# A macaron network on one core: KAN input made once and copied by transfers, rotated query by transfers, one ring of PSUM banks

## The chip, the cores and the metric

The kernel runs on one core of one Trainium2 chip. The metric is the device time of one execution in microseconds (us); the time of the kernel before is the median of three runs. The engines that matter are PE (TensorE, matmuls), DVE (VectorE), ACT (ScalarE), POOL (GpSimd), and the queue SP, from which most transfers (DMAs) are issued, one after the other.

## The reference, cut to what matters

Sixteen sequences ("rows", b = 0 to 15) of 512 tokens with 128 features pass five residual blocks: a KAN block, causal attention with rotary positions, the same KAN block again, an expert block, and a recurrence with a second expert block. The change touches the first three.

```
x = x + 0.5 * ffn(layernorm(x))      # KAN
x = x + attn(layernorm(x))           # 16 query heads of 8, 4 key heads, causal
x = x + 0.5 * ffn(layernorm(x))      # KAN

ffn:  s = x @ Win + bin               # 128 -> 64
      h = relu(s[..., None] * W1 + b1)   # 16 hidden values for each of the 64
      g = (h * W2).sum(-1) + b2
      out = g @ Wout + bout              # 64 -> 128
attn: q = x @ Wq;  q = q * cos + rotate_half(q) * sin
      rotate_half swaps the two halves of a head's 8 values and negates one
```

Every KAN needs each of its 64 inner features 16 times, with another slope and offset each time.

## The kernel before, in words

**Staging.** The program is a set of Python generators. Each `yield` ends a turn; `turn()` lets every live generator run one step and so fixes the order of the instructions on PE, DVE, ACT and POOL, which then run in that order. Only the SP queue is ordered by a scheduler. While a row runs (`paced`), a generator asks for room in the turn with `need(...)`, and `bank(...)` hands out one of two PSUM banks ("mm") for side work. Work appended to `later` is issued at the start of the next turn.

**The main loop** goes through rows b = -1 to 15 in 44 turns each: `weights(b)` makes the transposed scores of row b on PE (L713, tile `ps_st`), ACT takes their exponent (L716, `pt`) and POOL cuts the diagonal (L718); `maxima(b+1)` makes the scores of the next row (L649, `ps_sc`) and DVE takes their row maxima (L654, L659). `outputs` multiplies weights by values (L739, `ps_av`). Beside these, as side work, run `stage_in(b+2 and on)` (first KAN, then `attn_in`: query, key and value) and `stage_out(b-1)` (output product, second KAN, gate scores). Row -1 has maxima alone. Before it stands a prologue: loads, KANs of rows 0 to 2, `attn_in` of rows 0 and 1. Behind row 15 come 512 products of experts (L1026 `ps_h`, L1039 `ps_y`, L990 `acc`), a PE-filled stage of some 660 us, with `recurrence` beside it.

**`kan(b)`.** After `norm` (DVE statistics, POOL power, transposes L338, ACT copy L340 to `kan_xT`) it makes the input product twice, once for each half of the 64 features, with a weight `win` that holds the 32 columns four times side by side: one 128x512 float32 matmul for each half (L358, `ps_s`; two passes of PE each), copied by ACT to `kan_s0` and `kan_s1` (L361). So the 128 partitions hold 32 features four times. Eight ACT instructions (L377, `kan_h`) spread over 15 turns give two of the hidden values for 64 features each. Eight matmuls of 32 columns (L387, `ps_kg`) sum them, four column groups of PE side by side; then ACT copy (L393), product with `wout` (L401, `ps_ko`), sum on DVE (L402).

**`attn_in(b)`.** Two 128x512 matmuls give the query (L445, `ps_pa`, weight `wq`) and the query with each head's halves swapped (L451, `ps_pb`, weight `wqr`); DVE multiplies them by cosine and sine (L446, L452), POOL adds them (L467). `parts` splits the sum into three bf16 parts, which go to DRAM (L427, `qs`) and come back in the layout of the scores (L516, `qp`).

**PSUM.** Eight banks: two "mm", one `avp`, one `kap` and two `scp` for the maxima in turn, two `stp` for the weights. So the maximum in turn i waits for DVE to have read that of turn i-3, and the weight of turn i waits for ACT to have read that of turn i-2. In row 15 the weights use the two `scp` banks too. In the expert stage `kap` holds `ps_x`, `scp` `ps_h` and `stp` `ps_y`.

**SP's first transfers** in order: x of row 0 (L72), `win`, small weights, `rope` (L188), x of rows 1 to 15 (L72), `wo` (L195), `wlam` (L217), `wf` (L219), `wst` (L1082), and then the transfers of `attn_in`.

Of the kernel before, what the change touches and what calls it, by code (L numbers as in the profile page):

```python
# [17 lines left out]
P = 128  # L18
# [19 lines left out]
IN, OUT = 38, 8  # L38
LATE = 28
EP = 5  # L40
PLACES = 8
# [7 lines left out]
def tile_macaron(  # L49
# [55 lines left out]
    with ExitStack() as ph:  # L105
# [8 lines left out]
        avp = ph.enter_context(tc.tile_pool(name="p1_av", bufs=1, space=PSUM))  # L114
        kap = ph.enter_context(tc.tile_pool(name="p1_ka", bufs=1, space=PSUM))
        scp = ph.enter_context(tc.tile_pool(name="p1_sc", bufs=2, space=PSUM))
        stp = ph.enter_context(tc.tile_pool(name="p1_st", bufs=2, space=PSUM))
        qkp = ph.enter_context(tc.tile_pool(name="qk", bufs=1))
# [6 lines left out]
        nc.vector.tensor_scalar_add(center, ident, -1.0 / D)  # L125
        win = cst.tile([D, 2, NI, MH], F32, name="win")
        binc = cst.tile([P, 2], F32, name="binc")
# [8 lines left out]

        for half in range(2):
            cols = win_in[:, half * MH : (half + 1) * MH]
            nc.sync.dma_start(out=win[:, half, :, :], in_=cols.unsqueeze(1).to_broadcast([D, NI, MH]))
        inner(kw1, kw1_in)  # L140
# [38 lines left out]

        wq = cst.tile([D, NH, HD], F32, name="wq")  # L180
        nc.sync.dma_start(out=wq, in_=wq_in.rearrange("k (h d) -> k h d", d=HD))
        wk = cst.tile([D, 2, HD, NR], F32, name="wk")
# [4 lines left out]
        rope = cst.tile([P, 2, S], F32, name="rope")  # L187
        nc.sync.dma_start(out=rope, in_=rope_in)  # L188
        out_weights()
# [6 lines left out]
        hh = HD // 2  # L196
        wqr = cst.tile([D, NH, HD], F32, name="wqr")
        identb = cst.tile([P, P], BF16, name="identb")
# [59 lines left out]

        held, kan_held, hurry = [0], [0], [False]

        def bank(shape, dtype, name, work=0.0):
# [8 lines left out]
        def freed():  # L270
            held[0] -= 1
# [77 lines left out]
        def kan(b):  # L349

            _, xT = yield from norm(x[b])
            sk = []
            for half in range(2):
                while half and kan_held[0]:
                    yield
                kan_held[0] |= half
                ps = yield from bank([P, S], F32, "ps_s", 0.9)
                nc.tensor.matmul(ps, lhsT=win[:, half, :, :].rearrange("d i m -> d (i m)"), rhs=xT,  # L358
                                 start=True, stop=True)
                sh = (w1p if half else w2p).tile([P, S], F32, name=f"kan_s{half}")  # L360
                later.append(lambda sh=sh, ps=ps: nc.scalar.copy(sh, ps))  # L361
                yield
                take(act=0.6)
                freed()
                sk.append(sh)
            yield

            hs = []
            begin = now[0]
            U = 2 * NV  # L370
            for t in range(U):
                while now[0] < begin + 15 * t // 8:
                    yield
                yield from need(act=0.8, **({"pool": 1.25} if t == 1 else {}))
                half, v = t // 2 % 2, t // 4 * 2 + t % 2
                h = hp.tile([P, S], F32, name="kan_h")
                nc.scalar.activation(h, sk[half], AF.Relu, bias=rbias[:, half, v : v + 1],  # L377
                                     scale=kw1[:, half, v : v + 1])
                hs.append((half, v, h))
                if t == 1:  # L380
                    nc.gpsimd.tensor_tensor(x[b], x[b], kcst.unsqueeze(1).to_broadcast([P, NT, D]), ALU.add)
                yield
            pg = yield from bank([P, S], F32, "ps_kg", 1.0)
            for begins in (True, False):
                for half, v, h in hs[0:4] if begins else hs[4:8]:
                    o = half * M + v % 2 * MH
                    nc.tensor.matmul(pg[o : o + MH, :], lhsT=w2d[:, half, v, :], rhs=h,  # L387
                                     start=begins, stop=not begins)
                if begins:
                    yield  # L390
                    yield from need(pe=1.0)
            gT = w2p.tile([P, S], F32, name="kan_g", tag="kan_s0")
            later.append(lambda: nc.scalar.copy(gT, pg))  # L393
            kan_held[0] = 0
            yield
            take(act=0.6)
            freed()
            yield
            po = yield from bank([P, NT, D], F32, "ps_ko", 0.9)
            for c in range(NT):  # L400
                nc.tensor.matmul(po[:, c, :], lhsT=gT[:, bass.ts(c, P)], rhs=wout, start=True, stop=True)  # L401
            later.append(lambda: nc.vector.tensor_add(x[b], po, x[b]))  # L402
            yield
            take(dve=0.7)
            freed()
            yield
# [16 lines left out]
        def spread(part, heads, name):  # L423

            scr = tc.dram_tile([3, HD, heads, S], BF16, name=name)
            for i in range(3):
                nc.sync.dma_start(out=scr[i].rearrange("d h t -> h d t"), in_=part[:, i, :])  # L427
            return scr
# [8 lines left out]
        def attn_in(b, st):  # L437
            _, xT = yield from norm(x[b])
            ka = w1p.tile([P, 2, P], F32, name="rope_ka")
            ta = w1p.tile([P, S], F32, name="rope_a")  # L440
            tb = w1p.tile([P, S], F32, name="rope_b", tag="yT")
            qpart = w1p.tile([P, 3, S], BF16, name="qpart")
            kpart = w1p.tile([P, 3, P], BF16, name="kpart")
            pa = yield from bank([P, S], F32, "ps_pa", 0.9)
            nc.tensor.matmul(pa, lhsT=wq.rearrange("k h d -> k (h d)"), rhs=xT, start=True, stop=True)  # L445
            later.append(lambda: nc.vector.tensor_mul(ta, pa, rope[:, 0, :]))  # L446
            yield
            take(dve=0.7)
            freed()
            pb = yield from bank([P, S], F32, "ps_pb", 0.9)  # L450
            nc.tensor.matmul(pb, lhsT=wqr.rearrange("k h d -> k (h d)"), rhs=xT, start=True, stop=True)  # L451
            later.append(lambda: nc.vector.tensor_mul(tb, pb, rope[:, 1, :]))  # L452
            yield
            take(dve=0.7)
            freed()
            pkv = yield from bank([P, 3, P], F32, "ps_kv", 1.3)
# [8 lines left out]
            yield  # L465
            yield from need(pool=1.25)
            nc.gpsimd.tensor_tensor(ta, ta, tb, ALU.add)  # L467
            take(dve=0.4)
# [16 lines left out]
            freed()  # L485
            st["va"] = va
            if paced[0]:
                yield
# [40 lines left out]
        def center_win():  # L529
            psc = yield from bank([P, 2 * NI * MH], F32, "ps_kc0")  # L530
            centered(psc, win.rearrange("d a i m -> d (a i m)"))
            freed()
# [10 lines left out]
        def prepare():  # L543
# [24 lines left out]
            psc = yield from bank([P, 3, P], F32, "ps_kc3")  # L568
            centered(psc[:, 0, :], wq.rearrange("k h d -> k (h d)"))
            centered(psc[:, 1, :], wk[:, 0, :, :].rearrange("k d h -> k (d h)"), wk[:, 0, :, :])  # L570
            centered(psc[:, 2, :], wv)
            freed()
            yield
            nc.vector.tensor_copy(wqr[:, :, 0:hh], wq[:, :, hh:HD])
            nc.vector.tensor_copy(wqr[:, :, hh:HD], wq[:, :, 0:hh])
            nc.vector.tensor_copy(wk[:, 1, 0:hh, :], wk[:, 0, hh:HD, :])
# [40 lines left out]
        def stage_in(b, st):  # L617
            late = b in through
            yield from kan_in(b)
            for _ in range(LATE if late and b > 2 else 0):  # L620
# [6 lines left out]
                 (1, (0, 1)), (1, (2, 3)), (0, (0, 1, 2, 3))]  # L627

        def in_bank(ps, gs):
            return ps.rearrange("p (u w) -> p u w", w=S // len(gs))  # L630

        turns = [0]

        def maxima(b, st):
            qp, kp = packed(b)
            for half in range(2):
                maxs = topped[half][:, 0 : NT * NH // 2].rearrange("p (h c) -> p h c", c=NT)
                for r in (2 * half, 2 * half + 1):
                    for c, gs in BANKS:
                        n = (c + 1) * P  # L640
                        v = in_bank((kap if turns[0] % 3 == 2 else scp).tile([P, S], F32, name="ps_sc"), gs)
                        turns[0] += 1
                        alone = len(gs) == 1
# [52 lines left out]
        def weights(b, st):  # L696
# [3 lines left out]
            for r in range(NR):  # L700
                pt = ptp.tile([P, NG, 1280], F32, name="pt")
                st["pt"][r] = pt
                for i, (c, gs) in enumerate(BANKS):
                    c = NT - 1 - c
                    n = S - c * P

                    if b == B - 1 and (r * len(BANKS) + i) % 2:
                        ps = scp.tile([P, S], F32, name="ps_sl", tag="ps_sc")
                    else:
                        ps = stp.tile([P, S], F32, name="ps_st")  # L710
                    v = in_bank(ps, gs)
                    for u, g in enumerate(gs):
# [231 lines left out]
        def dispatch():  # L944
            while taken[0] < NR * B:
                yield
            for i in range(0, len(order), 2):
# [4 lines left out]

                ps = kap.tile([D, 2, CAP], F32, name="ps_x", tag="ps_sc")
                for j in range(2):
# [6 lines left out]
        def experts():  # L961
# [55 lines left out]
            while begun[0] < len(order) or any(line) or rounds:  # L1017
                now = None
                if begun[0] < moved[0]:
# [3 lines left out]
                    begun[0] += 1  # L1023
                    pst = scp.tile([P, NF, CAP], F32, name="ps_h", tag="ps_sc")
                    for f in range(NF):
# [5 lines left out]
                if line[1]:  # L1031
                    k, b, e, u = line[1]
                    g, n = b // GB, (b % GB) * E + e
                    if prod[1]:
                        v = place[k, b, e]
                        nc.vector.tensor_scalar(sels[v], iota, tokT[g][:, n : n + 1], None, ALU.is_equal)  # L1036
                    py = stp.tile([CAP, D], F32, name="ps_y", tag="ps_st")
                    for f in range(NF):
# [273 lines left out]
```

## Time and profile before

| what | value |
|---|---|
| three runs | 1592.62, 1592.74, 1594.12 us; median 1592.74 us |
| the profiled execution | 1585.11 us, span of its instructions 1583.1 us, mean granted PE clock 0.984 |
| busy share of the span | PE 93%, weight loads 66%, DVE 69%, ACT 61%, POOL 58% |
| prologue and row -1, 0 to 110.88 us | up to the first exponent of row 0 |
| rows 0 to 15, 110.88 to 913.11 us | rows 5 to 9 take about 52 us each |
| expert stage, 920 to 1583 us | PE 99% busy up to 1440 us |
| L358 `ps_s`, 128 passes | 71.1 us busy, 644 ns each |
| L361 copies of `ps_s`, 64 | 37.5 us busy, 586 ns each |
| L451 `ps_pb`, 32 passes | 17.5 us busy, 628 ns each |

The times of rows are those between the first exponents of successive rows in the timeline. A line of the profile names the line of the kernel, the engine, and the tiles written and read; "idle" is the time in which the engine had nothing running before an instruction, with what released it. The end of a matmul is modelled, so the distance between the starts of successive matmuls tells more than their durations do.

### The profile page before, as it was taken

To read this page: it belongs to the slowest core of one execution; us is meant where nothing else is said; L and a number is where in the kernel's file an instruction comes from. 1 tells how busy PE (TensorE), PEld (TensorE's weight loads), DVE (VectorE), ACT (ScalarE), POOL (GpSimd) and SP (SyncE) were. 2 spreads that over 40 slices of the span, in tenths; PEclk is the share of its full clock that TensorE was granted. 3 is DMA by queue.
4 is the path that set the end of the run, shared out by engine and by line. 5 is a ranking of instruction groups with operands and counts; after the bars stand their busy time and mean duration, and the time that the engine had idled before them with its cause. 6 is when DMAs were issued, how large, how long until landed. Compare 5 with 4: busy or idle time off the path is not lost.

```text
span 1583.1 us, 33175 instructions
## 1 busy us (share of the span) xinstructions
PE 1479.8 (93%) x11902; PEld 1045.6 (66%) x11905; DVE 1085.0 (69%) x3574; ACT 960.5 (61%) x1852; POOL 922.7 (58%) x1439
## 2 busy tenths in 40 slices
PE   4689989999999999999999899999999999999997
PEld 2334454455445454445444489999998999999997
DVE  5587877878788788888888345765569665753333
ACT  3445767777778777777776865444454444544443
POOL 2535545555555564556454766667666666767773
PEclk9889999999999999999999999999999999999998
DMA  5220110122111210221122113223332332333332
GB/s 136 81 58 30 58 52 13 50 59 60 36 33 53 60 52 12 58 60 35 30 79 68 50 45 70 60 57 73 72 73 59 72 72 63 81 64 67 69 67 60
DMA packets 107466, 92.87 MB, mean 59 GB/s; under 512 B 23469, under 2 KB 95862, under 8 KB 107062
## 3 DMA queue, kind: packets, MB, share of 16 engines
q1 hardware_dynamic: 84464, 67.67, 15.0%
q0 software_dynamic: 21584, 22.89, 7.8%
q8 instruction: 93, 1.52, 0.4%
q14 instruction: 71, 0.58, 0.1%
q10 hardware_dynamic: 1254, 0.20, 0.1%
HBM read 59.20 MB, written 35.45 MB: 60 GB/s over the span
## 4 chain that ended last, share of the span: by engine, by line
PE 76%; DVE 10%; ACT 7%; issue 2%; DMA 2%; POOL 1%; SPq 1%; ACTq 0%; DVEq 0%; POOLq 0%
PE ps_h L1026 13%; PE ps_y L1039 13%; PE ps_av L739 9%; PE ps_st L713 7%; PE ps_sc L649 5%; PE acc L990 5%; PE ps_kg L387 4%; ACT pt L716 4%; PE ps_s L358 3%; DVE below L654 3%; ACT kan_h L377 2%; PE ps_t L338 2%; PE ps_x L955 2%; DVE topped L659 2%; PE ps_g L800 2%
## 5 line engine op out<-in xcount | busy, mean ns | idle before, releaser
L716 ACT ACTIVATE pt<-ps_st 128x512 f32<-128x512 f32 x682 | 369.9, 566 | 126.3 <-PE ps_st L713 124.6
L718 POOL TENSOR_SCALAR_AFFINE_SELECT pt<-pt 128x128 f32<-128x128 f32 (+2 forms) x704 | 250.9, 365 | 320.4 <-ACT pt L716 314.4
L654 DVE CUSTOM_DVE_ANT_0 below<-ps_sc,causal 128x512 bf16<-128x512 f32 (+1 forms) x512 | 315.6, 616 | 106.5 <-PE ps_sc L649 91.0
L935 POOL DMA_INDIRECT xg<-xnd,tokI x256 | 252.8, 988 | 82.9 <-issue 37.8
L1028 ACT ACTIVATE mo<-ps_h 128x512 f32<-128x512 f32 x256 | 152.8, 597 | 217.7 <-PE ps_h L1026 217.4
L713 PE MATMUL ps_st<-qp,kp 128*128 128x512 bf16 (+1 forms) x990 | 247.6, 301 | 33.2 <-ACT pt L716 30.7
L1026 PE MATMUL ps_h<-xin,mw 128*128 128x128 f32 x2048 | 272.5, 276 | 0.0
L1039 PE MATMUL ps_y<-mw,mo 128*128 128x128 f32 x2048 | 270.8, 275 | 0.0
L649 PE MATMUL ps_sc<-kp,qp 96*128 96x512 bf16 (+3 forms) x1024 | 256.6, 304 | 5.9 <-DVE topped L654 3.9
L1026 PEld LDWEIGHTS ps_h<-xin,mw 128*128 128x128 f32 x2048 | 250.3, 192 | 12.4 <-issue 9.9
L1039 PEld LDWEIGHTS ps_y<-mw,mo 128*128 128x128 f32 x2048 | 249.4, 192 | 1.0 <-DVE ye L1036 0.8
L713 PEld LDWEIGHTS <-kp 128*128 128x128 bf16 x1024 | 94.9, 100 | 183.9 <-issue 164.7
L377 ACT ACTIVATE kan_h<-kan_s,rbias,kw 128x512 f32<-128x512 f32 x256 | 207.6, 821 | 0.0
L1056 POOL DMA_INDIRECT sum<-mo,tokI x93 | 152.1, 1635 | 69.7 <-issue 26.7
L739 PE MATMUL ps_av<-pt,va 128*32 128x512 f32 (+3 forms) x2048 | 164.6, 439 | 1.0 <-POOL pt L718 0.7
L649 PEld LDWEIGHTS <-qp 96*128 96x128 bf16 x1024 | 95.9, 99 | 87.4 <-issue 64.7
L659 DVE TENSOR_REDUCE topped<-ps_sc 128x2 f32<-128x512 f32 (+1 forms) x192 | 127.0, 683 | 23.1 <-PE ps_sc L649 22.8
L739 PEld LDWEIGHTS ps_av<-pt,va 128*32 128x32 f32 x2048 | 53.3, 109 | 85.4 <-issue 42.7
L312 POOL TENSOR_TENSOR ln_rstd<-ln_rstd,mhalf 128x4 f32<-128x4 f32 x96 | 102.4, 1067 | 8.0
L311 POOL TENSOR_SCALAR ln_rstd<-ln_mv 128x4 f32<-128x4 f32 x96 | 21.9, 228 | 138.1 <-DVE ln_mv L309 137.7
L1045 DVE SCALAR_TENSOR_TENSOR ye<-ps_y,gainT,ye 128x128 fp32r<-128x128 f32 x83 | 29.0, 349 | 84.7 <-ACT ye L1042 84.4
L1045 DVE SCALAR_TENSOR_TENSOR parts<-ps_y,gainT,parts 128x128 fp32r<-128x128 f32 x80 | 27.9, 349 | 83.9 <-ACT parts L1042 83.8
(204 smaller groups left out, 2296.5 us busy)
## 6 DMA issues: line engine op xcount, KB each, us to landing
qp<-qs SPq DMA_DIRECT2D x64, 288.0 KB
xnd<-kan_x SPq DMA_DIRECT2D x32, 256.0 KB
sum<-x SPq DMA_DIRECT2D x62, 128.0 KB
qs<-qpart SPq DMA_DIRECT2D x48, 128.0 KB
kp<-ks SPq DMA_DIRECT2D x48, 96.0 KB
x<-in_L_attn_x_dram SPq DMA_DIRECT2D x16, 256.0 KB
mw<-in_L_ffn_w_dram SPq DMA_DIRECT2D x16, 256.0 KB
xg<-xnd,tokI POOLq DMA_INDIRECT x256, 2.5
```

What stands on the lines that cost most here:

```text
L377: nc.scalar.activation(h, sk[half], AF.Relu, bias=rbias[:, half, v : v + 1], scale=kw1[:, half, v : v + 1])
L649: nc.tensor.matmul(v[:, u, 0:n], lhsT=qp[r][0:MXR, g, bass.ts(c, P)], rhs=kp[0:MXR, r, 0:n], start=alone, stop=(u == len(gs) - 1), skip_gr ...
L654: nc.vector.tensor_tensor_reduce(below[:, 0:n], v[:, 0, 0:n], causal[:, S - n : S], 1.0, LOWEST, ALU.add, ALU.max, accum_out=maxs[:, h, c ...
L659: nc.vector.tensor_reduce(maxs[:, h : h + len(gs), c], v[:, :, 0:n], AX.X, ALU.max)
L713: nc.tensor.matmul(v[:, u, 0:n], lhsT=kp[ROWS, r, bass.ts(c, P)], rhs=qp[r][ROWS, g, c * P : S], start=True, stop=True)
L716: nc.scalar.activation(o, v[:, :, 0:n], AF.Exp, scale=HD ** -0.5)
L718: nc.gpsimd.affine_select(out=dg, in_=dg, compare_op=ALU.is_ge, fill=0.0, base=0, pattern=[[0, len(gs)], [1, P]], channel_multiplier=-1)
L739: nc.tensor.matmul(po[32 * g : 32 * g + 32, c * P : S], lhsT=va[:, c, r, :], rhs=pt[:, g, OFF[c] : OFF[c] + n], start=(c == 0 and not odd) ...
L935: nc.gpsimd.indirect_dma_start(out=xgs[i // E % 2][:, i % E, :], out_offset=None, in_=xnd[b], in_offset=bass.IndirectOffsetOnAxis(ap=tokI[ ...
L1026: nc.tensor.matmul(pst[:, f, :], lhsT=mw1[e][:, bass.ts(f, P)], rhs=xins[i // E % 2][:, i % E, :], start=True, stop=True)
L1028: nc.scalar.activation(hs[u], pst, AF.Gelu)
L1039: nc.tensor.matmul(py, lhsT=hs[u][:, f, :], rhs=mw2[e][:, f, :], start=(f == 0), stop=(f == NF - 1))
```

## The change

Three edits.

1. **KAN input.** `win` holds the 64 columns once. Four matmuls of 32 columns and 256 tokens write the 64 features for the two halves of the tokens to the four column groups of one bank, [128, 256]; one ACT copy takes it to `kan_m`; two transfers write it to DRAM (`kn`), two transfers read it back, each with the 32 features of one half four times. `kan` lets some turns pass in between (`REST = 3` of them behind the reads). The two reads now both wait until no other KAN holds `kan_s` (before, only the second half did).
2. **Rotated query.** The columns of `wq` are ordered by place in the head, then head, so the two halves of all heads stand on the two sides of the partitions. `ps_pb` and `wqr` go. DVE multiplies `ps_pa` by the sine into `turned_` (in the place of `qpart`) and by the cosine into `ta`; two transfers bring the two sides of `turned_` crosswise to `tb`; POOL adds a few turns later than before. `rope` is loaded by four transfers, with each row repeated for the heads.
3. **Banks.** The five banks of maxima and weights become one ring in the order of issue. A weight now follows in the bank of the maximum three turns earlier, a maximum in that of the weight two turns earlier. In the expert stage each tile has a bank of its own number, two for `ps_h`, two for `ps_y`, one for `ps_x`, as before.

```
         def kan(b):
             _, xT = yield from norm(x[b])
+            ps = yield from bank([P, S // 2], F32, "ps_s", 0.75)
+            for half in range(2):
+                for th in range(2):
+                    o = th * M + half * MH
+                    nc.tensor.matmul(ps[o : o + MH, :], lhsT=win[:, half * MH : (half + 1) * MH],
+                                     rhs=xT[:, th * S // 2 : (th + 1) * S // 2], start=True, stop=True)
+            sm = w1p.tile([P, S // 2], F32, name="kan_m")
+            later.append(lambda: nc.scalar.copy(sm, ps))
+            yield
+            take(act=0.4)
+            freed()
+            scr = tc.dram_tile([2, MH, S], F32, name=f"kn{len(kns)}")
+            kns.append(scr)
+            for th in range(2):
+                nc.sync.dma_start(out=scr.rearrange("a m t -> (a m) t")[:, th * S // 2 : (th + 1) * S // 2],
+                                  in_=sm[th * M : (th + 1) * M, :])
+            yield
+            while kan_held[0]:
+                yield
+            kan_held[0] = 1
+            yield
             sk = []
             for half in range(2):
-                while half and kan_held[0]:
-                    yield
-                kan_held[0] |= half
-                ps = yield from bank([P, S], F32, "ps_s", 0.9)
-                nc.tensor.matmul(ps, lhsT=win[:, half, :, :].rearrange("d i m -> d (i m)"), rhs=xT,
-                                 start=True, stop=True)
                 sh = (w1p if half else w2p).tile([P, S], F32, name=f"kan_s{half}")
-                later.append(lambda sh=sh, ps=ps: nc.scalar.copy(sh, ps))
-                yield
-                take(act=0.6)
-                freed()
+                nc.sync.dma_start(out=sh, in_=scr[half].unsqueeze(0).to_broadcast([NI, MH, S]))
                 sk.append(sh)
-            yield
+            for _ in range(REST):
+                yield
...
         def attn_in(b, st):
...
-            nc.tensor.matmul(pa, lhsT=wq.rearrange("k h d -> k (h d)"), rhs=xT, start=True, stop=True)
-            later.append(lambda: nc.vector.tensor_mul(ta, pa, rope[:, 0, :]))
+            nc.tensor.matmul(pa, lhsT=wq.rearrange("k d h -> k (d h)"), rhs=xT, start=True, stop=True)
+            turned_ = qpart.rearrange("p i t -> p (i t)")[:, 0 : 2 * S].bitcast(F32)
+            later.append(lambda: nc.vector.tensor_mul(turned_, pa, rope[:, 1, :]))
             yield
             take(dve=0.7)
-            freed()
-            pb = yield from bank([P, S], F32, "ps_pb", 0.9)
-            nc.tensor.matmul(pb, lhsT=wqr.rearrange("k h d -> k (h d)"), rhs=xT, start=True, stop=True)
-            later.append(lambda: nc.vector.tensor_mul(tb, pb, rope[:, 1, :]))
-            yield
-            take(dve=0.7)
-            freed()
+            yield from need(dve=0.7)
+            nc.vector.tensor_mul(ta, pa, rope[:, 0, :])
+            freed()
+            tb = w1p.tile([P, S], F32, name="rope_b", tag="yT")
+            for a in range(2):
+                nc.sync.dma_start(out=tb[halves[a], :], in_=turned_[halves[1 - a], :])
...
+        NB = 5
+        turns = [0]
+        def next_bank(shape, name):
+            turns[0] += 1
+            return scp.tile(shape, F32, name=name, tag=f"bank{turns[0] % NB}")
```

## The prediction

> **What bounds the kernel now.** I read the windows by stage first, then the chain of waits inside one steady row, then the waits of rows 4 to 12, and last the timeline of SP, ACT and DVE in the first 40 us. The window of one row (its columns: length, then busy time and count for PE, weight loads, DVE, ACT, POOL, then clock, DMA share, GB/s) and the waits of 319 to 793 us (total, times, longest):
>
> ```profile
> 372.00:424.00 52.00, 49.61 (x401) 25.66 (x399) 41.01 (x138) 40.72 (x75) 27.09 (x61) 1.00 0.15 43
> ...
> ACT pt L716 <- PE ps_st L713: 62.5, 95, 1.4
> DVE below L654 <- PE ps_sc L649: 55.5, 92, 1.1
> ...
> PE ps_st L713 <- ACT pt L716: 19.9, 42, 0.9
> ```
>
> The reader is to see that ACT and DVE wait for PE (62.5 and 55.5 us), PE for ACT only 19.9 us: in a row PE is the bound, with ACT and DVE a fifth below it. The DMA engines are 15% busy and can carry more. The chain of the same row says what PE's pieces cost when others queue behind them (start, length, piece):
>
> ```profile
> 374.40 0.91 PE ps_s L358 x2
> ...
> 376.18 0.98 PE ps_s L358 x2
> ...
> 410.75 0.91 PE ps_pa L445 x2
> ...
> 412.09 0.86 PE ps_pb L451 x2
> ...
> 418.92 1.00 PE ps_kg L387 x8
> ```
>
> Two passes of a 128x512 product hold PE for 0.86 us (0.43 each). Eight passes of 32 columns with 512 tokens hold it for 1.00 us: four lie side by side, so two rounds of 0.43 and 0.14 on top. In the expert stage PE is 99% busy and the change touches one KAN there.
>
> **KAN product (gain).** A KAN loses four passes, 4 x 0.43 = 1.72 us of PE, and gets eight passes of 32 columns and 256 tokens: two rounds of half of 0.43, plus the same 0.14, 0.57 us. Saved: 1.15 us. The Trainium skill, "TensorEngine Tiling (Array Packing)", Key Properties, says against such a step that a change of tiling mode drains TensorE; the 0.14 us above is all that this case shows of it, and by it the gain is the same sum. Of 32 KANs, five begin in the prologue or row -1 and one runs in the expert stage; 26 lie in rows 0 to 15: **-30 us**, and -1 for the one among the experts.
>
> **ps_pb (gain).** 0.86 us of PE for each row; three of 16 lie ahead of row 0: 13 x 0.86 = **-11 us**. DVE keeps both multiplications (0.68 us each), so it gains nothing. What is late next in these turns is ACT or DVE; both have a fifth to spare.
>
> **ACT copies.** Two of 0.586 us become one of 128x256 (nearest row, L957 on ACT: 0.368): 0.80 us of ACT less for each KAN. ACT is covered by PE, so I cost it at nothing; where ACT ends last, up to -10 us over the rows.
>
> **The KAN's new wait.** The first of eight ACT instructions (L377) now waits for a write to DRAM and a read. Queued behind it on ACT are the exponents of the row, and PE's next scores wait for those. In the turn counters of the two programs the first L377 stands five turns behind the copy; at 52/44 = 1.18 us that is 5.9 us of cover. The way: copy 0.37, two issues on SP at 0.5 (L434: 0.55), landing of the write, issue of the read 0.4 to 0.8, landing of the read. For a landing the nearest rows are these (SP's queue, start and length):
>
> ```profile
> 391.82 0.33 SPq L688 DMA_DIRECT2D ms<-mr  x1
> 393.69 0.56 SPq L690 DMA_DIRECT2D qp<-ms  x2
> ...
> 201.81 4.85 DMA qp<-qs
> ```
>
> L690 reads what L688 wrote, and is issued 1.87 us after it began: 1.5 us of landing. 4.85 us is a read of 288 KB when four of them run at once. So a read of 256 KB lands in 1.5 to 4.85 us; I take 3, nearer to the lone transfer, since the row's DMA share is 0.15. Sum: 0.37 + 1.0 + 1.5 + 0.6 + 3 = 6.5 us, 5.0 to 8.3 by the bounds. It is 0.6 us late, and up to 2.4. The banks let PE run about two turns ahead, so I take 0.3 us of each as lost: 26 x 0.3 = **+8 us** (0 to 60; see the first rival). The page "DMA: Bandwidth & Descriptors", Anatomy of one DMA, gives about 2.0 us fixed for each transfer plus the bytes at 436 GB/s; by it, as an estimate, the two landings are 2.2 and 2.6 us, 6.8 us in all, and the lost time would be nearly the same.
>
> **Rotation by transfers.** The sum on POOL (L467) waits for two transfers of 128 KB; no instruction of the scores waits for it, since the query is needed a row later, and SP's L516 waits for the banks of the old query (SP: 51.8 us for PE `ps_st`) and not for its data. Nothing in the rows. SP gets ten issues more for each row (about 5 us of 52) and has the room.
>
> **The ring.** A weight no longer waits for ACT's last but one exponent; the maximum behind it does. PE's 19.9 us of waiting for ACT in nine rows can shrink by the length of one score product (0.22 us x 42 times, 9 us) at most; the new wait of a weight for DVE is 0.2 us earlier than the maximum's was. **-3 us** (-10 to +6).
>
> **Prologue (loss).** SP issues in order, and the built order of the changed kernel puts the first `kn` write behind all loads. The timelines of SP, ACT and DVE before:
>
> ```profile
> 24.28 5.70 SPq L195 DMA_DIRECT2D wo<-in_L_attn_Wo_dram  x8
> 30.08 1.17 SPq L217 DMA_DIRECT2D wlam<-in_L_attn_W_lam_dram  x2
> 31.30 0.58 SPq L219 DMA_DIRECT2D wf<-in_L_attn_W_F_dram  x1
> ...
> 18.75 0.58 ACT L361 COPY kan_s<-ps_s 128x512 f32<-128x512 f32 x1 [0.94 <-PE ps_s L358]
> 19.24 5.75 ACT L377 ACTIVATE kan_h<-kan_s,rbias,kw 128x512 f32<-128x512 f32 x8
> ...
> 31.64 0.68 DVE L402 TENSOR_TENSOR x<-ps_ko,x 128x512 f32<-128x512 f32 x1
> ```
>
> Row 0's copy is done near 18 us, but SP is free at 31.9. Then two issues 1.0, landing 1.5, issue 0.4, landing 3: `kan_s0` is there at 37.8 us instead of 19.2, **18.5 us late**. All four engines run in order, so the rest of the prologue hangs on it. L402 had 3.6 us of slack (its product ended at 28.0, it ran at 31.64 behind the statistics of rows 1 and 2): 15 us are left. On top: one transfer hop in each of two `attn_in` where `ps_pb` stood on the chain (2 x (3 - 1.7), some +2), and row 2's second read, which stands in SP behind the query loads of row 0 (about 5 us behind its turn): +5. Off: two `ps_s` pairs on the chain at 1.1 (-2), fewer products in row -1, whose end DVE sets (-3). **+17 us** (+10 to +24).
>
> **Sum.** Against the profiled 1585.1 us: -30 - 11 - 1 + 8 - 3 + 17 = -20, so 1565. The median of the runs stands 7.6 us above that execution; on its scale 1592.7 - 20 = **1573 us**.
>
> **Rivals.** *A, the copy is late in every row (slower).* For: SP waits up to 24.7 us for DVE (L688), so a KAN transfer behind one is late, and ACT is in order; against: the built order puts such transfers only behind others of about the same turn. Place: the first L377 of each KAN. Price: at 8.3 us or a blocked queue, each KAN loses about 2.2 us behind the two turns of cover: 26 x 2.2 = 57 instead of 8, 1573 + 49 = 1622. Without this term the sum is -28, so it decides from 28/26 = 1.1 us lost for each KAN. *B, the gain of PE is half real:* ACT and DVE (41 us of 52) become the end of the turns; for: a fifth of the row's chain is already ACT; against: the waits above. Then -21 instead of -41: 1593, no change. *C, the prologue hides the late copy* (row 1's loads land at 26 us, DVE clears buffers meanwhile): 1573 - 17 = 1556. Against: the in-order engines. *D, the 32-column products don't lie side by side:* 8 x 0.215 = 1.72 us, no gain in the KAN: 1573 + 31 = 1604. Against: L387's eight passes in 1.00 us.
>
> **Chances.** Forecast 0.55 (faster but for 0.02 within the bound), A 0.15 (slower), B 0.15 (a third each way), C 0.10 (faster), D 0.05 (slower). Faster by over 0.2% (3.2 us, about what a measurement of this kernel can tell from no change): 0.53 + 0.05 + 0.10 = 0.68; within 0.07; slower 0.15 + 0.05 + 0.05 = 0.25. Range: down to 1547 (C with ACT's 10 us), up to 1606 (D, and the milder part of A); beyond lie about 0.15 above and 0.05 below. The forecast's own range is 1558 to 1588.
>
> **What would show it.** Right: L358 at 0.57 us of PE for each KAN, rows 5 to 9 at about 49.5 us instead of 52, the first L377 at 38 us, row 0's first exponent near 128 us instead of 110.9, waits of L377 for a transfer under 1 us in the rows. Wrong: rows still at 52 us (B), long waits of ACT L377 for `kn` with PE waiting for ACT behind them (A), row 0 at 111 (C).

## The result, and the profile after

| | before | after |
|---|---|---|
| median of four runs | 1592.68 us (1590.84 to 1594.12) | 1704.96 us (1698.82 to 1710.3) |
| ratio | | 1.0705, 95% interval 1.0673 to 1.0737 |
| profiled execution; span | 1585.11; 1583.1 us | 1704.64; 1702.6 us |
| mean granted PE clock | 0.984 | 0.944 |
| prologue and row -1 | 110.9 us | 151.9 us |
| rows 0 to 15 | 802.2 us, clock 0.996 | 874.1 us, clock 0.932 |
| what follows (expert stage) | 670.0 us | 676.6 us |

The changed kernel is 7% slower, where 1.2% faster was forecast. Of the 119.5 us between the two spans 41.0 lie ahead of row 0, 71.9 in the rows and 6.6 behind them. The groups on the page of the kernel after that changed most (busy us and mean ns, then the idle us ahead of them and what ended most of it), and the queue of SP's transfers (packets, MB, share):

```profile
q1 hardware_dynamic: 99808, 92.75, 18.7%
...
L668 PE MATMUL ps_sc<-kp,qp 96*128 96x512 bf16 (+3 forms) x1024 | 269.1, 319 | 62.6 <-ACT pt L731 59.1
...
L392 ACT ACTIVATE kan_h<-kan_s,rbias,kw 128x512 f32<-128x512 f32 x256 | 207.0, 816 | 151.8 <-DMA kan_s<-kn 150.8
```

L392 is the KAN's hidden value (L377 before). ACT stood 150.8 us idle ahead of it, for the read of the copied input; before, nothing waited there. And PE waited for ACT ahead of its maxima. The same in rows 0 to 15 alone, in the waits of the kernel after (us in total, times, longest):

```profile
ACT pt L731 <- PE ps_st L728: 127.6, 159, 3.0
DVE below L673 <- PE ps_sc L668: 116.5, 144, 5.3
ACT kan_h L392 <- DMA kan_s<-kn: 85.2, 32, 9.6
```

and in PE's own list of waits there:

```profile
PE ps_sc L668 <- ACT pt L731: 59.1, 35, 5.2
PE ps_sc L664 <- ACT pt L731: 21.8, 17, 9.5
PE ps_st L728 <- DVE topped L673: 12.9, 27, 0.8
```

In the rows of the kernel before, PE's longest wait in total was another one, for the bank of a weight:

```profile
PE ps_st L713 <- ACT pt L716: 30.7, 66, 0.9
```

85.2 us of ACT for the transfer, 80.9 us of PE for ACT ahead of the maxima: they are nearly the same number, and the timeline of one KAN shows why (start, length, engine, instruction; in brackets the idle time ahead of it and what ended it):

```profile
482.25 0.37 ACT L361 COPY kan_m<-ps_s 128x256 f32<-128x256 f32 x1 [0.33 <-PE ps_s L358]
...
483.43 1.11 SPq L368 DMA_DIRECT2D kn<-kan_m  x2
...
487.50 1.13 SPq L378 DMA_DIRECT2D kan_s<-kn  x2
...
488.86 0.49 ACT L731 ACTIVATE pt<-ps_st 128x384 f32<-128x384 f32 x1 [1.32 <-PE ps_st L728]
...
489.65 0.32 PE L728 MATMUL ps_st<-qp,kp 128*128 128x384 bf16 x1
...
492.29 0.81 ACT L392 ACTIVATE kan_h<-kan_s,rbias,kw 128x512 f32<-128x512 f32 x1 [2.94 <-DMA kan_s<-kn]
493.01 0.47 ACT L731 ACTIVATE pt<-ps_st 128x384 f32<-128x384 f32 x1
...
493.53 0.48 PE L668 MATMUL ps_sc<-kp,qp 96*128 96x384 bf16 x1 [3.56 <-ACT pt L731]
```

The copy on ACT ends at 482.62; the first hidden value can start at 492.29, 9.7 us later, of which 4.8 us lie behind the issue of the reads. ACT takes its instructions in order, so the exponents behind L392 wait too, no bank comes free, and PE stands still for 3.56 us. And behind the gap PE is slow: the L668 of 384 columns takes 0.48 us, 0.32 ahead of it (at 489.40). Two windows of the kernel after show it by the clock (length, then busy time and count for PE, weight loads, DVE, ACT, POOL, then granted clock, DMA share, GB/s):

```profile
490.00:500.00 10.00, 5.54 (x26) 3.62 (x26) 5.66 (x19) 6.06 (x11) 4.29 (x10) 0.64 0.44 132
500.00:540.00 40.00, 35.66 (x288) 17.67 (x288) 28.25 (x92) 27.13 (x52) 14.03 (x37) 0.92 0.18 50
```

In the rows of the kernel after, the clock's record has 21 stretches at 0.50, 119.5 us together, and PE 31 idle gaps of over 1 us, 85.2 us together; before, there was one such stretch of 6.8 us and four gaps of 6.6 us. In the prologue the first copy stands where the prediction put it, behind the loads of SP, and later than it said. SP's timeline and ACT's, of the kernel after:

```profile
15.94 12.02 SPq L73 DMA_DIRECT2D x<-in_L_attn_x_dram  x15
28.00 5.28 SPq L197 DMA_DIRECT2D wo<-in_L_attn_Wo_dram  x8
33.38 1.18 SPq L218 DMA_DIRECT2D wlam<-in_L_attn_W_lam_dram  x2
34.60 0.58 SPq L220 DMA_DIRECT2D wf<-in_L_attn_W_F_dram  x1
35.28 1.11 SPq L368 DMA_DIRECT2D kn<-kan_m  x2
```

```profile
43.44 1.52 ACT L392 ACTIVATE kan_h<-kan_s,rbias,kw 128x512 f32<-128x512 f32 x2 [25.70 <-DMA kan_s<-kn]
...
63.21 1.52 ACT L392 ACTIVATE kan_h<-kan_s,rbias,kw 128x512 f32<-128x512 f32 x2 [5.11 <-DMA kan_s<-kn]
...
84.37 1.52 ACT L392 ACTIVATE kan_h<-kan_s,rbias,kw 128x512 f32<-128x512 f32 x2 [7.32 <-DMA kan_s<-kn]
95.04 1.52 ACT L392 ACTIVATE kan_h<-kan_s,rbias,kw 128x512 f32<-128x512 f32 x2 [9.15 <-DMA kan_s<-kn]
```

### The profile page after: what moved, and what is told of

It reads as the page before. It is cut to its first block, busy times and chain, and to the rows that moved or that the text cites. A ratio compares the mean times of both kernels' runs of the same rounds, so it can differ in the third digit from the quotient of the medians.

```text
span 1702.6 us, 33670 instructions
## 1 busy us (share of the span) xinstructions
PE 1474.6 (87%) x11988; PEld 1041.1 (61%) x12001; DVE 1087.7 (64%) x3572; ACT 939.0 (55%) x1820; POOL 918.1 (54%) x1439
## 5 line engine op out<-in xcount | busy, mean ns | idle before, releaser
L733 POOL TENSOR_SCALAR_AFFINE_SELECT pt<-pt 128x128 f32<-128x128 f32 (+2 forms) x704 | 246.6, 357 | 412.0 <-ACT pt L731 405.8
L731 ACT ACTIVATE pt<-ps_st 128x512 f32<-128x512 f32 (+1 forms) x704 | 374.8, 562 | 139.9 <-PE ps_st L728 127.6
L668 PE MATMUL ps_sc<-kp,qp 96*128 96x512 bf16 (+3 forms) x1024 | 269.1, 319 | 62.6 <-ACT pt L731 59.1
L392 ACT ACTIVATE kan_h<-kan_s,rbias,kw 128x512 f32<-128x512 f32 x256 | 207.0, 816 | 151.8 <-DMA kan_s<-kn 150.8
L728 PE MATMUL ps_st<-qp,kp 128*128 128x512 bf16 (+3 forms) x1011 | 261.0, 315 | 24.7 <-DVE topped L673 12.9
L1071 POOL DMA_INDIRECT sum<-mo,tokI x93 | 152.2, 1636 | 71.9 <-ACT mo L1043 32.2
L754 PE MATMUL ps_av<-pt,va 128*32 128x512 f32 (+3 forms) x2048 | 174.0, 459 | 0.7 <-POOL pt L733 0.7
L668 PEld LDWEIGHTS <-qp 96*128 96x128 bf16 x1024 | 100.7, 104 | 81.1 <-issue 51.6
L314 POOL TENSOR_TENSOR ln_rstd<-ln_rstd,mhalf 128x4 f32<-128x4 f32 x96 | 102.5, 1068 | 8.0
L402 PE MATMUL ps_kg<-kan_h,w2d 128*32 128x512 f32 x512 | 81.7, 630 | 24.6 <-ACT kan_h L392 23.2
L340 PE MATMUL ps_t<-ident,kan_x 128*128 128x128 f32 x384 | 67.0, 305 | 37.8 <-DVE kan_x L328 19.7
```

The lines of the kernel that those rows point to most:

```text
L668: nc.tensor.matmul(v[:, u, 0:n], lhsT=qp[r][0:MXR, g, bass.ts(c, P)], rhs=kp[0:MXR, r, 0:n], start=alone, stop=(u == len(gs) - 1), skip_gr ...
L728: nc.tensor.matmul(v[:, u, 0:n], lhsT=kp[ROWS, r, bass.ts(c, P)], rhs=qp[r][ROWS, g, c * P : S], start=True, stop=True)
L731: nc.scalar.activation(o, v[:, :, 0:n], AF.Exp, scale=HD ** -0.5)
L733: nc.gpsimd.affine_select(out=dg, in_=dg, compare_op=ALU.is_ge, fill=0.0, base=0, pattern=[[0, len(gs)], [1, P]], channel_multiplier=-1)
L754: nc.tensor.matmul(po[32 * g : 32 * g + 32, c * P : S], lhsT=va[:, c, r, :], rhs=pt[:, g, OFF[c] : OFF[c] + n], start=(c == 0 and not odd) ...
L1071: nc.gpsimd.indirect_dma_start(out=sums[k, b], out_offset=bass.IndirectOffsetOnAxis(ap=tokI[g][:, n : n + 1], axis=0), in_=added[b % 2 * ( ...
```

## The experiments

Theory 1: the KAN's copies come late; ACT stands in order, PE runs dry behind it, and its clock falls. Theory 2, the rival: the one ring of banks, which ties the maxima to ACT's exponents, is what makes PE wait. The eleven kernels ran in three groups. Each ratio is against the kernel before, run on the same chip beside it (medians there 1630.61, 1592.76 and 1602.12 us); the chip of the first group is some 38 us slower, by its traces nearly all of it in the expert stage (706 to 718 us there, 670.0 in the trace of before). Stages are therefore compared for the prologue and the rows alone, and with the one trace of before.

| kernel | ratio, 95% interval | prologue | rows 0 to 15 | PE busy there | PE idle there | clock there | ACT waits for `kan_s` there |
|---|---|---|---|---|---|---|---|
| before | 1 | 110.9 | 802.2 | 748.5 | 53.7 | 0.996 | 0 |
| after | 1.0705 | 151.9 | 874.1 | 742.8 | 131.3 | 0.932 | 85.2 |
| kan_alone | 1.0726, 1.0696 to 1.0756 | 146.0 | 886.7 | 756.9 | 129.8 | 0.925 | 89.4 |
| rope_alone | 0.9961, 0.9945 to 0.9976 | 117.4 | 798.2 | 738.7 | 59.5 | 0.993 | 0 |
| ring_alone | 0.9936, 0.991 to 0.9961 | 109.5 | 801.0 | 751.7 | 49.3 | 0.989 | 0 |
| no_kan | 0.9964, 0.995 to 0.9978 | 116.9 | 800.8 | 743.4 | 57.4 | 0.987 | 0 |
| rest6 | 1.0414, 1.0375 to 1.0453 | 152.8 | 830.3 | 725.8 | 104.5 | 0.971 | 30.5 |
| late_loads | 1.0688, 1.0651 to 1.0725 | 140.0 | 875.3 | 746.2 | 129.1 | 0.930 | 84.7 |
| mixed6 | 1.0187, 1.0149 to 1.0225 | 115.2 | 826.1 | 723.6 | 102.5 | 0.977 | 25.7 |
| one_hop | 1.0881, 1.0838 to 1.0923 | 161.2 | 892.8 | 752.3 | 140.5 | 0.926 | 105.9 |
| less_pe | 0.994, 0.992 to 0.9959 | 115.6 | 795.6 | 733.1 | 62.5 | 0.985 | 0 |
| kan_late5 | 1.0234, 1.0212 to 1.0255 | 124.1 | 823.4 | 738.3 | 85.1 | 0.998 | 0 |
| no_ring6 | 1.0454, 1.0432 to 1.0476 | 152.6 | 829.2 | 722.9 | 106.3 | 0.973 | 27.8 |

"PE idle" is the length of the rows less PE's busy time; some records of matmuls can be missing, so it is good to a few us.

### The three edits apart

*kan_alone* is the kernel before with edit 1 (the lines of `win` and of `kan` in the diff above), *rope_alone* with edit 2 (`wq`, `rope`, `attn_in`, no `wqr`), *ring_alone* with edit 3 (`next_bank` and its users), *no_kan* with edits 2 and 3.

> The kernel before with the KAN part of the change alone (old rotation, old banks). Theory 1 (late copy: the two hops of the KAN input take 8 us where five turns cover 6, ACT stands at its first hidden value, PE behind ACT, and the clock falls in the gaps; and the first copy stands behind all loads): nearly the whole loss is here, 1680 to 1710 us, prologue some 35 us longer, rows some 55 us a row. Theory 2 (the ring is to blame, since it ties the maxima of DVE to the exponents of ACT): without the ring a late copy costs little, 1610 to 1640 us.

> The kernel before with the rotation by transfers alone. Theories 1 and 2 both: 11 us of PE less in the rows, 3 to 10 us more in the prologue, 1580 to 1598 us. If the 41 us by which the prologue grew are the rotation's as much as the KAN's: 1600 to 1615 us.

> The kernel before with the ring of five banks alone. Theory 1: 1583 to 1597 us, PE's waits for ACT no longer than the 31 us of before. Theory 2: over 1600 us, with PE waiting for ACT at the maxima (L649) by some 50 us more.

> The changed kernel without the KAN part (rotation by transfers and ring stay). Theory 1: the loss is gone, 1575 to 1600 us, clock at 0.98 again. Theory 2: 1610 us or more.

The KAN's edit alone makes the whole loss (1.0726, after 1.0705); without it the rest is 0.4% faster than before. Theory 2 falls: the ring alone is 0.6% faster than before, and with the ring and the rotation beside the KAN the rows are shorter than with the KAN alone, 874.1 against 886.7 us. *ring_alone* is faster than both kernels and has the lowest ratio of this study, but its interval overlaps those of *rope_alone*, *no_kan* and *less_pe* below.

### More cover, and the loads out of the way

*rest6* gives the reads three turns more:

```
-REST = 3
+REST = 6
```

> Three turns more between the issue of the KAN's reads and their first use: eight turns of cover instead of five, 8 x 1.18 = 9.4 us against the 8.1 us from the copy to the first hidden value that the changed kernel showed in undisturbed rows. Theory 1 (the copy comes late, ACT stands in order, PE runs dry and its clock falls): the 85 us of ACT waiting for the transfer in the rows fall below 15, PE's waits for ACT from 90 to under 35, the clock in the rows goes from 0.93 to 0.98 or more, and the rows from 874 to 765-785 us. The prologue stays 40 us longer than in the kernel before, for the first copies still stand behind the loads: ratio 0.99-1.01. Theory 2 (the one ring of banks ties maxima and weights to ACT, and the KAN only shows it): ACT's waits for the transfer fall, but PE's waits for ACT stay near 60-90 us and the rows above 840: ratio 1.04-1.07.

Somewhat less than half of it came. The rows fell by 44 us, where 89 to 109 had been expected, ACT's waits for the transfer by 55 us, and the clock rose to 0.971: the late copy does cost what theory 1 says. But the rows stayed 28 us longer than before, not 17 to 37 us shorter, so theory 1 isn't the whole of it. Two places are left. In rows 2 to 9 ACT doesn't wait for the transfer at all, and yet they take 433.3 us (424.4 before, 449.2 after). In rows 11 to 15 they take 255.4 us (236.4 before): there copies are late again. The SP queue of rest6 at the worst of them, and ACT behind it:

```profile
794.78 1.11 SPq L368 DMA_DIRECT2D kn<-kan_m  x2
801.22 2.35 SPq L442 DMA_DIRECT2D qs<-qpart  x2
803.70 0.57 SPq L449 DMA_DIRECT2D ks<-kpart  x1
805.97 0.32 SPq L442 DMA_DIRECT2D qs<-qpart  x1
806.61 0.56 SPq L449 DMA_DIRECT2D ks<-kpart  x1
807.33 0.55 SPq L378 DMA_DIRECT2D kan_s<-kn  x1
```

```profile
823.49 0.81 ACT L392 ACTIVATE kan_h<-kan_s,rbias,kw 128x512 f32<-128x512 f32 x1 [10.55 <-DMA kan_s<-kn]
```

The write is issued 0.02 us after its copy, the first read 12.6 us behind it: it stands in SP's order behind five issues for the query and key of another row, of which the first waited 5.2 us for ACT's `qpart`. The second read followed at 816.75.

*late_loads* takes the loads of rows 3 to 15 out of the way of the first copy:

```
-        for b in range(1, B):
+        for b in range(1, 3):
             load(b)
...
+                if t == 0 and len(kns) == 1:
+                    for late in range(3, B):
+                        nc.scalar.copy(x[late][:, 0, 0:1], mhalf[:, 0:1])
+                        load(late)
```

> The rows' loads of x for rows 3 to 15 are issued on SP only behind row 0's first KAN (a copy of one column on ACT into each tile holds them back), so the first write of the KAN product no longer stands behind 13 loads. If the head of SP's queue makes the prologue's loss: the first hidden value of row 0 at 26-30 us instead of 43.4, and the prologue 137-142 us instead of 152; the rows as in the changed kernel (870-880 us), ratio 1.055-1.065. If the prologue's loss comes from the transfers themselves (two hops in each chain, and the later reads behind the query's): the first hidden value is earlier all the same, but the prologue stays at 148-152 us, ratio 1.07.

The first hidden value came at 31.6 us instead of 43.4 (26 to 30 had been expected), and row 0 began 11.9 us earlier; the rows stayed as they were (875.3). So by its trace the head of SP's queue is worth 12 us of the prologue's 41. The ratio doesn't show this by itself: 1.0688 stands beside the 1.0705 of the changed kernel with overlapping intervals, and its interval begins at 1.0651, just above the 1.055 to 1.065 that was expected.

*mixed6* makes the KANs of the prologue and of row -1 as the kernel before does, and has `REST = 6` for the others:

```
+            sk = yield from (spread_by_pe(xT) if filling[0] else spread_by_dma(xT))
```

(`spread_by_pe` holds the old two products with a weight of their own, `spread_by_dma` the new code.)

> KANs of the prologue and of row -1 make their product on PE in four copies, as the kernel before does; those of the rows and of the experts copy by transfers, with eight turns of cover. Theory 1: prologue 115-119 us (as the kernel with the rotation alone, 117.4), rows 765-785, tail as before: 25-35 us less than the kernel before, ratio 0.977-0.985, faster than both kernels. Theory 2: rows above 840, ratio 1.02 or more.

The prologue was as expected (115.2), the rows were not (826.1): again 24 us above before. ACT's 25.7 us of waiting for transfers, most of them late in the rows, are a part of that, but rows 2 to 9, with 1.0 us of such waits, take 434.4 us too (424.4 before). It doesn't beat the kernel before.

*one_hop* leaves out DRAM:

```
-            scr = tc.dram_tile([2, MH, S], F32, name=f"kn{len(kns)}")
...
-                nc.sync.dma_start(out=sh, in_=scr[half].unsqueeze(0).to_broadcast([NI, MH, S]))
+                for th in range(2):
+                    o = th * M + half * MH
+                    for i in range(NI):
+                        nc.sync.dma_start(out=sh[i * MH : (i + 1) * MH, th * S // 2 : (th + 1) * S // 2],
+                                          in_=sm[o : o + MH, :])
```

> The changed kernel, five turns of cover, but the copies go straight from the small tile to the large ones, sixteen transfers of 32 partitions by 256 tokens and no DRAM between: one landing instead of two, and 16 issues instead of four. Way to the first tile: 0.37 for the copy, eight issues at 0.5 and one landing of 1.5-2, so 5.9-6.4 us instead of 8.1; the second tile 4 us behind it, when its first use comes 2.8 us behind (four hidden values at 0.7). Theory 1 (the length of the way against the cover decides): ACT's waits for the transfer fall from 85 us to 20-50, the clock rises to 0.96-0.98, rows 800-840 us, ratio 1.02-1.05. Were it not the length but that a transfer stands on the way at all (any wait in ACT's order costs the same), the rows would stay at 870.

A miss: slower than the changed kernel, with more waiting (105.9 us). SP's and ACT's timelines of one KAN in one_hop:

```profile
355.37 2.51 SPq L377 DMA_DIRECT2D kan_s<-kan_m  x4
357.98 0.72 SPq L709 DMA_DIRECT2D qp<-ms  x2
358.74 7.49 SPq L377 DMA_DIRECT2D kan_s<-kan_m  x12
```

```profile
362.50 0.81 ACT L392 ACTIVATE kan_h<-kan_s,rbias,kw 128x512 f32<-128x512 f32 x1 [0.87 <-DMA kan_s<-kan_m]
...
368.82 0.81 ACT L392 ACTIVATE kan_h<-kan_s,rbias,kw 128x512 f32<-128x512 f32 x1 [3.67 <-DMA kan_s<-kan_m]
```

In this KAN the first tile is there 7.2 us after the copy's end (355.34) instead of some 8.5, but the sixteen issues take 10 us of SP, and the second tile, first used by the third hidden value, is now what is late (3.67). So issues took the place of the landing that was saved. It doesn't show what one landing alone would be worth; that more waiting goes with longer rows fits theory 1.

### What was left: the place of the KAN, and what PE's time is worth

For the rows that stay long without a wait for transfers there were two explanations. Theory 3: the place; with more turns between copy and hidden values the KAN's work comes to stand in worse turns. Theory 4: the relief of PE isn't worth its time, since ACT and DVE end the turns (rival B). And the ring (theory 2) had to be tried once more in this state. Each got a kernel.

*less_pe* is the kernel before with one input product less for each KAN (its second half copies the bank of the first, so the second half of the KAN's input is replaced by the first):

```
-                ps = yield from bank([P, S], F32, "ps_s", 0.9)
-                nc.tensor.matmul(ps, ...)
+                if half == 0:
+                    ps = yield from bank([P, S], F32, "ps_s", 0.9)
+                    nc.tensor.matmul(ps, ...)
```

> The kernel before, in which a KAN makes one of its two input products and both copies on ACT read it: the second half of the KAN's input is thereby replaced by the first. Nothing else is changed: no transfer, no ring. It takes 0.86 us of PE from each KAN and nothing from ACT or DVE. If a row is as long as PE's work (the forecast's step): 26 x 0.86 = 22 us off the rows, 802 to 780, ratio 0.984-0.989. If ACT and DVE set the turns as soon as PE is relieved (the rival of the half gain), 0-8 us: ratio 0.995-1.00, and PE's own idle time grows by what it was relieved of.

```profile
115.60:911.00 795.40, 732.89 (x5913) 376.37 (x5912) 625.30 (x2075) 596.25 (x1121) 439.40 (x953) 0.98 0.17 47
```

This window of less_pe is its rows. PE's busy time fell by 15.4 us, the rows by 6.6 us, and PE's idle time grew by 8.8 us. (The clock's record has four stretches at 0.5 here, 23.9 us together; a busy time at full clock would have fallen further, toward the 22.) By the ratio the gain of the whole kernel is 0.6% (0.4 to 0.8%), 10 us (7 to 13), and there 32 KANs lose 32 x 0.86 = 27.5 us of PE. So PE's time was worth about a quarter to a half of itself, 6.6 of 22 us in the rows and 7 to 13 of 27.5 in all. This may be somewhat low: *less_pe* also holds the product's bank until the second copy, longer than the kernel before does, and its prologue is 4.7 us longer than before although it only leaves work out.

*kan_late5* is no_kan, with the product on PE, and with five turns where no_kan has one between the KAN's last copy and its first hidden value; that is four turns more, not the five of the expectation below:

```
-            yield
+            for _ in range(5):
+                yield
 
             hs = []
```

> Rotation by transfers and the ring, KAN product on PE as in the kernel before, but with five turns more between the KAN's copies and its first hidden value, about where the kernel with eight turns of cover has it (that one showed no wait for the transfer in rows 2 to 9 and still 433 us for them, against 424 before and 423 in the kernel with rotation and ring). If the later place of the KAN's work in the row costs by itself (its norms and hidden values come to stand in the turns where a half row's maxima end): rows 2 to 9 at 430 us or more, ratio 1.005-1.015. If the place costs nothing: 420-425 us, ratio 0.994-1.000.

Rows 2 to 9 took 441.7 us (no_kan 422.5), and rows 3 to 8 became alike, 55.7 us each; all rows together grew by 22.6 us and the prologue by 7.3. No transfer stands on the KAN's way, the DMA share is 0.17 (0.16 before), and the clock is 0.998. So the later place costs by itself, and more than was expected. What PE waits for in rows 2 to 9 of kan_late5:

```profile
PE ps_t L340 <- DVE mr L690: 10.3, 7, 1.5
PE ps_t L340 <- ACT kan_xT L342: 8.4, 7, 1.2
PE ps_sc L656 <- ACT pt L719: 8.3, 21, 0.5
PE ps_sc L652 <- ACT pt L719: 6.6, 14, 0.5
PE ps_st L716 <- DVE topped L666: 6.5, 8, 0.9
PE ps_m L676 <- DVE topped L666: 3.6, 7, 0.5
```

The first two lines are the norms' transposes (L340), seven times each in these eight rows: they wait for the end of a half row's maxima on DVE (`mr`) and for ACT's copy of the transposes before them. In the same rows before, PE waited 16.6 us for ACT ahead of weights (L713) and at most 1.1 us for any of these; in no_kan the first two lines were 4.1 and 1.6 us. And rest6, whose copies come by transfers, has the same list in its rows 2 to 9:

```profile
PE ps_t L340 <- DVE mr L702: 10.3, 7, 1.5
PE ps_sc L668 <- ACT pt L731: 9.5, 23, 0.7
PE ps_t L340 <- ACT kan_xT L342: 7.6, 7, 1.2
PE ps_sc L664 <- ACT pt L731: 7.0, 15, 0.5
PE ps_st L728 <- DVE topped L678: 6.5, 8, 0.9
PE ps_m L688 <- DVE topped L678: 3.6, 7, 0.5
```

So what kept rest6's steady rows long is most likely the place of the KAN and not its transfers: the same waits come without any transfer. That rests on the likeness of the two lists, not on a run that moved the place back.

*no_ring6* is rest6 with edit 3 left out (the banks of before).

> The changed kernel with eight turns of cover and the kernel before's own banks for maxima and weights instead of the one ring. If the ring is what keeps the rows with eight turns long (PE waited 2.1 us for ACT there in each row, ahead of maxima): rows 2 to 9 below 425 us instead of 433, ratio below 1.036. If the ring helps beside the KAN as it did beside the five turns (887 against 874 us of rows): rows 835-850, ratio 1.045-1.055.

Rows 829.2 against 830.3 us, rows 2 to 9 431.7 against 433.3, ratio 1.0454 against 1.0414 with intervals that overlap. The ring is neither what keeps these rows long nor, as far as this shows, a help to them. The 887 and 874 us of the expectation differ by the rotation as well as by the ring.

## Why the prediction was wrong

**What failed: "The KAN's new wait", with its +8 us, and behind it "the banks let PE run about two turns ahead, so I take 0.3 us of each as lost".** It was rival A, with a price too small even there (2.2 us for each KAN). ACT waited 85.2 us for the 26 KANs of the rows, 3.3 us for each, and PE nearly as long behind it, where 0.3 us for each had been taken. Three things were off.

- *The way.* Forecast 6.5 us (5.0 to 8.3) against 5.9 of cover. Measured, for the 26 KANs of the rows: 8.5 us in the median from the copy's end to the first hidden value, 7.6 at least; with the copy's own 0.37, which the forecast counted, 8.8. The write was about right (2.8 us from its issue to that of the read); the read was not: 5.5 us from issue to use where 0.6 + 3 stood. Of the two rows between which the prediction chose, the upper one, a read of 4.85 us, was nearer. That row was also misread: SP's queue issued two reads of 288 KB and three of 96 KB there (from 200.89 us on), not four of 288 KB at once, so it was less of an upper bound than it seemed.
- *The banks.* They absorb nearly nothing: ACT waits 85.2 us for transfers in the rows, and PE 80.9 us for ACT ahead of its maxima, 86.9 with the weights, where no_kan, with the same ring, has 8.4.
- *The clock.* The prediction had no term for it. PE's busy time in the rows should have fallen by 41 us, to 707; it was 742.8. So some 35 us of slower matmuls came on top, by this subtraction, which is an estimate; the 119.5 us at half clock can have cost 60 at most.

The rows' 72 us follow: PE's idle time +77.6 us, its busy time -41 + 35. That the waits are the cause is shown by rest6 (55 us of waits less, 44 us of rows less) and by no_kan (no waits, 800.8 us).

**"KAN product" and "ps_pb" (-30, -11): right as work, wrong as time.** The product takes what was forecast; the chain of waits inside a row of rest6 has

```profile
466.76 0.57 PE ps_s L358 x8
```

and rope_alone shows PE 9.8 us less busy (748.5 to 738.7) with rows 4.0 us shorter. But less_pe puts the worth of PE's time at a quarter to a half: rival B, which the prediction gave 0.15 because ACT and DVE were only "a fifth below". Waits of ACT and DVE for PE show who ends most turns; they don't say that every turn shrinks with PE. By that, as an estimate, 41 us of PE would have been worth 10 to 20 had all else held.

**A term that was missing: the place.** Turns of cover were counted as free. The KAN, the second KAN and `attn_in` of a row follow one another through its 44 turns, so a later hidden value moves the next norm, and kan_late5 measures 22.6 us of rows for four turns. The changed kernel has fewer added turns than that, so a part of this is in its rows too; how much was not measured.

**Prologue: +17 forecast (+10 to +24), +41 measured.** The cause was named and the size was off. The write of row 0 was issued at 35.28 instead of 31.9, since the four loads of `rope` and the rest of SP's list had grown; its read landed 5.5 us after its issue instead of 3: 43.4 instead of 37.8. The two tiles of KAN 2, of which the second was taken at +5, cost ACT 7.3 and 9.2 us. KAN 1 and the KANs of row -1 wait as well, which the sum left out, and PE's clock is 0.71 to 0.72 from 70 to 152 us (0.89 from 20 to 70); but it was low before too, 0.83 from 20 to 70 and 0.79 from 70 to 110 us, so little of the loss can be the clock's. The edits apart give 35.1 us for the KAN and 6.5 for the rotation; late_loads takes 11.9 back. Each is from a single trace, and the 6.5 is not much more than the 4.7 by which less_pe's prologue grew.

**ACT copies (nothing), rotation in the rows (nothing), the ring (-3, -10 to +6):** in keeping with the runs. ACT's busy time fell by 16.5 us in the rows and no time came of it; the rotation's rows are 4 us shorter, not longer; the ring is worth 6 to 15 us by its ratio. Its trace doesn't show where: PE's waits for ACT in the rows fell from 32.2 to 10.4 us, yet rows and prologue are 1.2 and 1.4 us shorter, and the rest would lie in the expert stage, for which there is no trace of before from that chip.

Still open: why exactly the later place costs, and how much of the 72 us it makes. The waits of kan_late5 name the norms' transposes beside the end of the maxima, but no run moved them alone. What a single landing would be worth was not measured either, since one_hop paid for it in issues.

## What to carry to other kernels

A small piece of PE's work replaced by a write and a read through DRAM needs its whole way covered, 8.5 us here from the engine's copy to the first use, and the cover must be measured at the engine that waits in order: nearly each us it was late came out again as a us of PE, here with a slower clock behind it. Before counting the gain, take the work away for one run and see what the time does: 27.5 us of PE were worth 7 to 13 us here. And turns inserted to hide a transfer are themselves a change of order, with a price of their own.

## What the runs showed of the hardware

**The clock often fell behind short gaps, but not behind all.** In the rows of the kernel after, each of the 21 stretches at a clock of 0.50 (3.4, 6.8, 10.2 or 13.7 us long) had an idle gap of PE of over 1 us begin in the 5 us ahead of it, and in 12 of them that gap was shorter than 3.4 us: 1.09 us idle from 554.6 us, then 6.8 us at half clock. The Trainium skill, "TensorE: Matmul & The Clock Gate", Part 1, says that the array goes to half speed after an idle window of about 3.4 us and that the window runs freely; its length agrees with the stretches, but the gaps ahead of them here were often of 1 to 3 us. No run set a gap by itself, so what decides stays open: in mixed6 four of eight stretches have no gap above 1 us ahead of them, and in kan_late5 19 gaps of over 1 us in the rows, 28.0 us together and 17 of them shorter than 1.5 us, went with a single stretch of 3.4 us.

**A read back from DRAM took longer than its bytes say.** The first of two reads of 256 KB, issued one behind the other: 4.8 us at least and 5.5 us in the median from issue to the first use, in rows with a DMA share of 0.23. The Trainium skill, "DMA: Bandwidth & Descriptors", Anatomy of one DMA, gives about 2.0 us fixed and 436 GB/s, an estimate of 2.6 us for it; but that section is on transfers issued from GpSimd, which the prediction didn't say, and these were issued from SP. The measured way decides.

**Order in the SP queue counts twice.** A read that is ready was issued 12.6 us after its write because five issues stood ahead of it, the first of which waited 5.2 us for ACT (rest6), and the first write of the kernel after was issued 17.5 us behind its copy (17.74 to 35.28).
